# A list-scheduled kernel for a convolution, a spectral mixer and an fp8 MLP: pieces' durations taken from the trace, and the order of issue searched anew

## The chip, the cores and the metric

The kernel runs on one core of a Trainium2 chip. The metric is the time of one execution on the device in microseconds (us). A core has five engines that run side by side, each with its own queue of instructions worked off strictly in order: PE (matrix multiplications, results into PSUM), DVE (vector work), ACT (activations and copies), POOL (a slower vector engine) and SP (issues most of the DMA transfers here). They wait for each other through semaphores. [...]

## The reference

The input is 32 images of 56 x 56 pixels with 96 channels. For each image `reference()` computes two layers, all with weights shared by the images.

Layer 0, a convolution block with mixed experts:

```python
pooled = jnp.mean(x, axis=(1, 2))
rw = jax.nn.sigmoid(pooled @ Wr + br)                     # 4 mixing weights per image
h = relu(bn(x @ Wk + ...))        # Wk = sum_e rw_e Wpw_e, 96 -> 384 channels
h = relu(bn(cond_dw(h)))          # sum_e rw_e * depthwise 3x3 convolution
x = bn(h @ Wk2 + ...) + x         # Wk2 = sum_e rw_e Wpwl_e, 384 -> 96 channels
```

Layer 1, on the 3136 pixels as tokens: `t + attn(layernorm(t))`, and then `t + ffn(layernorm(t))`. The attn is a map from 96 to 192 channels with relu, an FFT over all 3136 tokens, a diagonal complex map with relu on the real and the imaginary part, the inverse FFT, its real part, and a map from 192 back to 96 channels. The ffn is a two-layer MLP (96 to 384 to 96) whose operands are rounded to an 8-bit float (5 exponent bits, 2 mantissa bits), with sums rounded to 16 bits.

## The kernel before

Every image is recorded by `record(b)` (line 767) as 572 small pieces of work, 118 of them on PE. A piece has an engine, an estimated duration, a due time, and the buffers and tiles that it reads and writes. `Plan.order()` (line 269) then runs a list scheduler over the pieces of all 32 images: whenever an engine of its model is free, it takes the ready piece with the earliest due time whose buffers can be had from their rings (PSUM banks are such a ring). The order in which pieces are taken is the order in which the program is written out (line 1477), and `Pinned` (line 370) keeps this order on every engine; so all instructions of the main part carry the line number 380. At run time the model's times have no meaning any more: an engine works off its queue in the written order and waits where an operand or a buffer isn't there yet.

What decides the order: `WANT` (line 173) with due times of the stages and the period between images, `NUDGE` (line 182), 572 numbers that are added to the due times, the same for every image, `HURRY` (line 176), subtracted from the due time of every DVE and ACT piece that reads PSUM, `LAG` and `DMA_LAG` (lines 156 and 162), the handoff times, `packets()` (line 165), the time of a transfer, and `slack`, a time by which a piece that reads a transfer is held back in the model after the transfer's modelled end. The order repeats from image to image once the pipeline is full; pieces of up to four images are interleaved.

The pieces of an image, by the names that this document uses (a number behind a name counts the pieces of that name within an image):

- *Convolution block.* `in` loads the image in four parts (SP), `pad` copies each into a padded tile (ACT). `route` (PE) makes the mixing weights; `wk`, `small` and `mix_wk2` (DVE) mix the expert weights, and `wd`, `wk2` rearrange them through DRAM (SP). The 384 channels are three chunks, the image two halves. Three of the six chunk-halves go "by vector": `expV` (PE), then nine taps as DVE and ACT pieces. The other three go "by tensor": `expT` (PE, four pieces), four transfers `hp` from SBUF to SBUF that regroup the channels, `conv` (line 990, PE, 64 matmuls in four phases), and four transfers `hid`. So there are `conv.0`, `conv.1` (first half) and `conv.2` (second half), with `hp.0` to `hp.11`. `proj.0` to `.2` and `.3` to `.5` (PE) project a half back to 96 channels, and `landed` (DVE) adds it to the image.
- *Forward part*, in four stretches of 14 rows: `turn` (PE transpose), `stats` and `rest` (DVE), `root` (line 1106, POOL) for the layer norm; `hidden` (PE), `scaled` (DVE), `along_h` (line 1173, PE, the transform along one axis), a copy on ACT, and transfers `gd` to DRAM. Each stretch has two groups, so there are `along_h.0` to `.7`.
- *Frequency part*, in seven groups of 4 or 5 frequencies: `g2` (line 1203) loads a group from DRAM, `along_q` (PE, two pieces per group) transforms along the other axis, nine pieces on ACT and DVE apply the diagonal map and the relu, `second` (line 1300, PE) maps 192 to 96 channels, `seconds` (ACT) copies it out, `back_q` (PE) transforms back, a copy, and `yd` stores it to DRAM.
- *Tail*, in four stretches again: `xs`, `yt`, `dd` are loads, `back_h` (line 1370, PE) transforms back along the first axis, which needs all seven `yd`; then `turn.4` to `.7`, `stats`, `rest`, `root` (POOL), `shift` (DVE), `normal` (line 1394, ACT), `turn_back` (line 1403, PE), a copy, and for each of three chunks `up` (line 1423, PE), a copy and a relu on ACT, a cast `h8` on POOL (line 1435), and `down` (PE); at last the sum and the store `out`.

Of the kernel before, what the change touches and what calls it, by code (L numbers as in the profile page):

```python
# [18 lines left out]
NE = 4  # L19
C = 96  # L20
# [144 lines left out]
def packets(n, size):  # L165
# [6 lines left out]

WANT = dict(period=113.9, half=60.1, expand=0.0, vector=1.4, forward=10.7, forward_step=27.0, freq=172.2,
            freq_step=7.0, tail=259.2, tail_step=26.5, x=17.0, mix=33.5, project=33.0)

HURRY = 666.0

# [4 lines left out]
NUDGE = [  # L182
    -172.8, -9.2, -163.5, -60.3, 106.2, -144.5, 5.2, 53.2, -138.8, -8.2, -18.1, 99.5, 147.5, 94.2, 30.4, 67.4, 92.4, -148.5,
    -6.5, -38.5, 17.2, -12.9, -15.4, -66.7, 8, 47.3, 43.1, -21, 54, 5.1, 79, 62.9, 70.9, 46, 65.8, 61.6,
    84.4, 85, 84.4, 40.6, -2.1, 87.1, 20.9, 22, 0.2, 78.2, 60.5, 28.6, 19, 81.3, 37.6, 57.2, 88.1, 56.4,
    66.3, 27.8, 87.7, 47.1, 3.9, -118.2, -64.2, -84.3, -87, 1.7, 38, -13.3, 3.3, 79.4, -68.9, 6.1, -39.3, -22.4,
    -19.6, 33.1, 71.9, 22.4, 90.3, 8.3, 105.6, -2.6, 53.5, -90.3, -62.6, -103.8, -44.5, 28.1, 84, 81.8, 41.1, 65.4,
    8.5, -38.6, -23.9, -6.9, 6.4, 31.1, 20.5, -24.2, -49.9, -25.7, -1.2, 35.9, 4.4, 29.3, 35.4, 31.7, 11.2, 32.7,
    -0.6, 2.9, 64.3, 55.4, 21.5, 6, 26.4, -13.2, -2.6, -11, -7.5, -46.8, -15.5, -65, -6.8, -1.4, -9.5, -61.2,
    -31.8, -58.5, 20.3, 11.2, -20.3, -4.1, -1.5, -38.9, -22.4, 22.3, 23.7, -10.1, 25.5, 18, -0.4, 34.1, 24.9, 15.9,  # L190
    16.3, -10.2, 31.4, 20, 22.3, 21.4, 68.6, 6.5, 20.6, 32.1, 45.3, 0.2, 87.8, 97.5, 26.2, 165.3, 25.8, 69.2,
    -2.3, 75.7, -13.1, 128.9, -49.1, -108.2, -48.2, -13.1, 8.1, -3, 25.2, 64.8, 93.3, -26.5, -18, -36.1, -44, 25,
    40.1, 17.9, -68.7, -67.4, -63.8, -83.2, 48.6, -63, 51.9, -62.9, 51.9, 52.1, -44.3, -24.4, -95.9, 11.6, 10.1, -125.8,
    -87.7, -2.9, -83.3, 1.2, -12.6, -52.9, -15.4, 74.6, -82.7, 30.3, -7, 42.3, 39.1, -114.4, 9.2, -95.3, 27.5, 21,
    -15.1, 18.2, 13.7, -47.5, 10, 15.9, -62.4, -63.7, 18.7, -75.9, 1.4, -102.1, 66, 13.6, -89.4, -47.9, -79.5, 7.9,
    27.8, -78.8, -48.7, -13.9, -80.9, 7.2, -17, -75.7, 2.9, 34.7, -79.6, 18.7, -29.5, -51.1, 29.1, -120.2, -27, -174.8,
    -19.6, -1.7, -101.7, -132.1, -25.7, -135.5, -3.1, -29.4, -68.3, -35, -106.8, -36.1, -32.9, -24.2, -19.8, -72.9, -51.2, -26.6,
    -193.3, -161, -26, -32.5, -13, -23, 2, -38.4, -26.7, -48.1, -139.2, -94.1, -29.8, -21.3, -65.4, -22.5, -55.3, -54.9,
    -104, 2.6, 50, -62.3, -1.2, -99.1, -50, -31.3, -93.3, -124, -30.2, 30.5, -6.3, -48.4, 9.1, -63.1, 23.9, -32.4,
    -123.4, -98.1, -13.4, -29.5, 2.9, -15.5, -54.1, -85.5, -81.5, -70, -65.3, -64.4, -9.9, -63.4, -67.9, -49.2, -238.5, -138.2,  # L200
    -51.4, -18.7, -39.4, -87.4, -30.3, -73.9, -33.3, -80.2, -229.8, -126.4, -52, -64, -103.4, -40.4, -65.3, -50.3, -83.5, -2.5,
    -2.7, -75.9, -43, -126.9, -9.5, -24.2, -129.6, -23.3, 4.8, 37.3, 44.5, 14.3, 64.3, -80.5, 24.6, -6, -141, -113.4,
    -0.5, -18.6, 6.6, -17.9, -90.6, -142.3, -89.1, -9.7, 39.2, 0.3, 64.2, -29.5, 14.3, 27.4, -160.3, -34.4, 20.7, 9.1,
    18.6, 19.1, 34, -87.3, 22.2, -20.8, -79.3, -114.3, -21, -1.7, -46.5, 1.5, -56.6, -68.3, -96, -11.4, 7.3, -31,
    -1, -113.3, -20.1, -2.5, -133.2, -104.9, -6.8, 32.5, -0.9, 15.3, 67.8, -62.8, 32.2, -0.4, -84, -89.1, 48.2, -11,
    9.3, 43.2, -1.5, -48, -40.4, 3.9, 40.7, -28.9, 46.7, -47.5, 12.9, 24.6, -140.4, -106.2, 23.3, 13.5, -12.4, 27.8,
    13.9, -47.3, -7.4, 5.3, -87, -93, 11.7, 18.1, -83.2, -13.4, -87, -74.7, 14.1, 53.6, 39.4, 15.6, -33.3, 7,
    -90, -14.5, -32.6, -58, -68.1, -127.6, 70.6, -91.1, -82, -120.2, -128, -95.6, -46.5, -198.2, -126.4, -74.2, -83.7, -138.5,
    -99, -84.9, -60.2, -28.1, 23.8, -92.6, 27.3, -29.5, -3, 14.7, 11.8, 22.6, 27.2, -37.4, -126.3, -32, -88.4, -49.7,
    -80.9, -115.3, 44.8, -36.2, -64.3, -126.9, -78.2, -25.2, -36.4, -46, -79, -23.3, -32.1, -93.1, -97.6, -15.3, -44.1, 7.2,  # L210
    69.9, -69, -43.9, 51.1, 2.7, 75.7, 49.8, 54.4, 62.2, -32.2, -53.4, 7.7, -51.1, -6.4, 24.5, -84.8, 136.4, -14.6,
    6.6, -88.3, -65, 0.9, -18.3, -70.5, -45.5, 2.6, -12.9, -65.1, -65.4, -0.1, -18.6, -23.2, 77.8, -37.1, 0.8, -7.6,
    5, 67.2, 25.4, 103.6, 150.3, 33.5, -55.5, 40.7, -47.9, 2.3, 49.7, -3.5, 176, 13.2, -18.2, -66.6, -65.7, -28.6,
    15.8, -58.1, 11, 16.7, -29, -88, -20.9, 33.5, -35.4, 17.5, 44.4, -13.1, 48.4, 59.1,
]
# [3 lines left out]
class Plan:  # L219
# [15 lines left out]

    def add(self, eng, dur, due, emit, reads=(), writes=(), takes=(), size=0, port=None):
        op = Op()
# [4 lines left out]
        op.eng, op.dur, op.due, op.emit = eng, dur, round(due, 3), emit  # L242
        op.takes, op.size, op.slack = list(takes), size, 0.0
        op.port = eng == "POOL" if port is None else port
# [141 lines left out]
def kernel(  # L386
# [56 lines left out]
    wpw_s = const([C + 1, NE + 1, M], F32, "wpw_s")  # L443
# [45 lines left out]
    with tc.tile_pool(name="prep", bufs=1) as pp:  # L489
# [4 lines left out]
        half = temp([128, 16], "half")  # L494
# [255 lines left out]
    add, move = plan.add, plan.move  # L750
# [16 lines left out]
    def record(b):  # L767
        t0 = b * PERIOD
        xh = [Buf(xr[h]) for h in range(2)]
        mix = Buf(r_mix)  # L770
        wk, small, wk2 = Buf(r_wk), Buf(r_small), Buf(r_wk2)
# [3 lines left out]
        for st in range(NS):  # L775
# [4 lines left out]
            else:  # L780
# [3 lines left out]
                    writes=[(sx, 0)], takes=[sx],  # L784
                )

            def pad(st=st, h=h, k=k, sx=sx):
# [6 lines left out]
            add(  # L794
                "ACT", 0.84, t0 - WANT["mix"] - 10 + 2 * st, pad, reads=[(sx, 0)], writes=[(xh[h], k), (mix, ("sum", st))],
                takes=[mix, *xh] if st == 0 else [],
            )
# [12 lines left out]
        def spread():  # L810
# [9 lines left out]
            reads=[(pooled, 0)], writes=[(psm, 0)], takes=[psm],  # L820
# [3 lines left out]
            reads=[(psm, 0)], writes=[(mix, 2)],  # L824
# [6 lines left out]
        def mixed(to, of, last, p):  # L831
            rw = mix.ap[0:p]
            for e in range(NE):
                ve.scalar_tensor_tensor(to, of[:, e], rw[:, e : e + 1], last if e == 0 else to, ALU.mult, ALU.add)

        def mix_wk2():
# [7 lines left out]
        add(  # L844
            "DVE", 3.08, t0 - WANT["mix"], lambda: mixed(wk.ap, wpw_s, wpw_s[:, NE], C + 1), port=True,
            reads=[(mix, 2)], writes=[(wk, 0)], takes=[wk],
# [3 lines left out]
            reads=[(mix, 2)], writes=[(small, 0)], takes=[small],  # L850
# [77 lines left out]
        def by_tensor(h, c, due, hid):  # L928
# [47 lines left out]
            def conv():  # L976
# [12 lines left out]
            add(  # L989
                "PE", 3.8, due, conv, reads=[(wg, 0), *((hp, r) for r in range(4))],  # L990
                writes=[(ps, r) for r in range(4)], takes=[ps],
# [83 lines left out]
        def moments(p, of, key, due, out_extra):  # L1075
# [29 lines left out]
            add("DVE", 0.52, due + 1, rest, writes=[(ln, 0)])  # L1105
            add("POOL", 1.78, due + 1, root, port=False, writes=[(ln, 0)])
            return ps, ln

        gd, yd, xd = Buf(r_gd), Buf(r_yd), Buf(r_xd)
        for st in range(NS):  # L1110
# [22 lines left out]
            for q0, nq in ((0, 4), (4, 3)):  # L1133
# [27 lines left out]
                def along_h(q0=q0, nq=nq, ps=ps, ha=ha, da=da):  # L1161
# [10 lines left out]
                add(  # L1172
                    "PE", 0.82, due + 3, along_h, reads=[(ha, 0), (da, 0)], writes=[(ps, 0)], takes=[ps, g],
                )
# [23 lines left out]
        for i, (k0, nk) in enumerate(GROUPS):  # L1198
# [6 lines left out]
                ),  # L1205
                reads=gd_parts, writes=[(g2, 0)], takes=[g2],
            )
# [80 lines left out]
            def second(nk=nk, nb=nb, ps=ps, za=zs[0], zb=zs[1]):  # L1288
# [10 lines left out]
            add(  # L1299
                "PE", 0.29 * nk + 0.1, due + 5, second, reads=[(zs[0], 0), (zs[0], 1), (zs[1], 0), (zs[1], 1)],  # L1300
                writes=[(ps, 0)], takes=[ps, zo],
# [38 lines left out]
        for st in range(NS):  # L1340
# [28 lines left out]

            add("PE", 1.43, due, back_h, reads=[(yt, 0), (dd, 0)], writes=[(ps, 0)], takes=[ps])  # L1370
            add(
# [21 lines left out]
            add("DVE", 0.1, due + 3, shift, writes=[(ln, 0)])  # L1393
            add("ACT", 2.1, due + 4, normal, reads=[(ps, 0), (ln, 0)], writes=[(nt, 0)], takes=[nt])
            ps, n8 = Buf(banks, 2), Buf(r_n8)
# [6 lines left out]

            add("PE", 0.55, due + 5, turn_back, reads=[(nt, 0)], writes=[(ps, 0)], takes=[ps, n8])
            add(
# [8 lines left out]
            for c in range(NC3):  # L1413
                ps, h16, h8 = Buf(banks, 2), Buf(r_h16), Buf(r_h8)

                def up(c=c, ps=ps, n8=n8):
# [5 lines left out]

                add("PE", 0.4, due + 7, up, reads=[(n8, 0)], writes=[(ps, 0)], takes=[ps, h16])
                add(
# [9 lines left out]
                add(  # L1434
                    "POOL", 0.79, due + 9.5,
                    lambda h16=h16, h8=h8: po.tensor_copy(h8.ap, h16.ap, saturate=False),
# [38 lines left out]
    for b in range(NB):  # L1475
        record(b)
    for op in plan.order():
        op.emit()


# [112 lines left out]
```

## Time and profile before

| | us |
|---|---|
| time before, median of 3 runs | 4395.16 (4389.32 to 4395.35) |
| profiled execution, its own time | 4390.8 |
| profiled execution, its span | 4389.0 |
| PE busy | 3988.9 (91%) |
| DVE busy | 3551.2 (81%) |
| ACT busy | 3110.9 (71%) |
| POOL busy | 1632.2 (37%) |
| main DMA queue, share of 16 engines | 64.8% |
| mean granted clock of PE | 0.950 |

A busy time is the time in which an engine worked on at least one instruction; the rest of the span it waited. The granted clock is the share of full speed at which PE was allowed to run: in a stretch at 0.5 a matmul takes twice its time, and the engine counts as busy meanwhile. A timeline line gives start, duration, engine, source line, operation, written and read tiles, shapes, the number of instructions in the group and, in brackets, the idle time before it with what ended it. All PE pieces come from line 380, so a piece is told by its tiles: `ps<-hp,wg` is `conv`, `ps<-dd,yt` is `back_h`, `ps<-ha,da` is `along_h`, `ps<-h,fw` is `down`.

### The profile page before, as it was taken

The page shows a single profiled execution, that of the slowest core. Times are in us where ns is not written, and L with a number is a line of the kernel's source. Part 1 is how long each engine was busy: PE and PEld are TensorE (multiplying, and loading weights), DVE is VectorE, ACT ScalarE, POOL GpSimd, SP SyncE. Part 2 cuts the span into 40 slices and gives each one's busy share as a digit, 9 for nine tenths or more (in the row PEclk, how much of TensorE's full clock was granted, in tenths as well). Part 3 has the DMA queues.
Part 4 walks back from the last instruction along what each step waited for, and adds up shares of the span by engine and source line. Part 5 has one row for each costly group of instructions (what it writes and reads, how often), then busy time and mean ns, then how long its engine had stood idle before and what let it go on. Part 6 is the DMA issues. An engine that isn't in the chain of part 4 may idle for free.

```text
span 4389.0 us, 104599 instructions
## 1 busy us (share of the span) xinstructions
PE 3988.9 (91%) x40066; PEld 2522.6 (57%) x40066; DVE 3551.2 (81%) x9036; ACT 3110.9 (71%) x6281; POOL 1632.2 (37%) x1332
## 2 busy tenths in 40 slices
PE   2888999999999999999999999999999999999985
PEld 0455655666565665655666655566565566665663
DVE  5877777798888889877888888888977888888853
ACT  1456766677777777766778777777876777877765
POOL 1223333333334434333333434433433333343333
PEclk9988999999999999999999999999999999999986
DMA  5754776666776666676666777666667666667642
GB/s 119 139 140 118 168 162 144 154 147 170 172 169 164 162 161 160 164 160 149 154 154 154 174 175 168 167 161 152 162 162 162 159 156 149 162 170 178 157 130 65
DMA packets 427749, 679.25 MB, mean 155 GB/s; under 512 B 155062, under 2 KB 290678, under 8 KB 427206
## 3 DMA queue, kind: packets, MB, share of 16 engines
q1 hardware_dynamic: 421632, 668.08, 64.8%
q8 instruction: 316, 5.18, 0.5%
q10 hardware_dynamic: 5618, 4.49, 0.4%
q14 instruction: 183, 1.50, 0.1%
HBM read 300.21 MB, written 211.04 MB: 116 GB/s over the span
## 4 chain that ended last, share of the span: by engine, by line
PE 46%; ACT 19%; DVE 13%; DMA 9%; POOL 6%; issue 4%; SPq 1%; POOLq 0%; ACTq 0%; DVEq 0%
PE ps L380 46%; ACT h L380 6%; ACT nt L380 5%; POOL ln L380 5%; DVE ln L380 3%; DVE ha L380 3%; ACT tmpa L380 2%; DMA hp<-h 2%; DMA yt<-yd 2%; DMA da<-dad 2%; DVE za L380 2%; DVE tmpa L380 2%; DVE h L380 1%; ACT tmpb L380 1%; ACT y L380 1%
## 5 line engine op out<-in xcount | busy, mean ns | idle before, releaser
L380 DVE SCALAR_TENSOR_TENSOR h<-h,small,h 128x784 f32<-128x784 f32 x1536 | 1557.0, 1050 | 103.3 <-ACT h L380 84.5
L380 POOL CAST h<-h 128x784 fp8e5<-128x784 f16 x384 | 511.2, 1335 | 738.3 <-ACT h L380 738.3
L380 PE MATMUL ps<-x,wk 97*32 97x435 f32 (+2 forms) x3840 | 698.7, 571 | 9.3 <-DVE wk L380 9.1
L380 POOL TENSOR_TENSOR ln<-ln,mhalf 120x7 f32<-120x7 f32 (+1 forms) x256 | 473.9, 1851 | 21.3
L380 PE MATMUL ps<-hp,wg 32*32 32x392 f32 x12288 | 420.4, 520 | 48.6 <-DMA hp<-h 28.1
L380 POOL TENSOR_SCALAR ln<-ln 120x7 f32<-120x7 f32 (+1 forms) x256 | 130.0, 508 | 866.4 <-DVE ln L380 866.4
L380 PE MATMUL ps<-dftb_s,g 112*128 112x112 f32 (+1 forms) x3776 | 432.1, 288 | 12.5 <-DVE tmpa L380 9.9
L380 ACT ACTIVATE h<-ps 128x435 f32<-128x435 f32 (+2 forms) x768 | 388.7, 543 | 69.8 <-PE ps L380 55.6
L380 PEld LDWEIGHTS ps<-dftb_s,g 112*128 112x128 f32 (+1 forms) x3776 | 353.3, 172 | 143.9 <-issue 41.9
L380 DVE SCALAR_TENSOR_TENSOR ha<-ps,ln,nshift 120x192 f32<-120x192 f32 x896 | 306.4, 408 | 155.7 <-PE ps L380 150.3
L380 DVE BATCH_NORM_STATS2 ln<-ps 120x6 f32<-120x96 f32 (+1 forms) x1792 | 315.8, 247 | 69.2 <-PE ps L380 68.5
L380 PEld LDWEIGHTS ps<-x,wk 97*32 97x32 f32 (+1 forms) x3840 | 203.6, 125 | 276.1 <-issue 141.9
L380 ACT ACTIVATE h<-h,fb 128x784 f16<-128x784 f16 x384 | 361.1, 965 | 1.3
L380 PEld LDWEIGHTS ps<-hp,wg 32*32 32x32 f32 x12288 | 218.7, 105 | 232.0 <-issue 106.9
L380 PE MATMUL ps<-w1c,x 96*120 96x192 f32 x1792 | 342.7, 342 | 6.6 <-issue 5.5
L380 ACT ACTIVATE nt<-ps,ln 112x96 fp8e5<-112x96 f32 x896 | 301.7, 436 | 62.6 <-DVE ln L380 58.7
L380 PEld LDWEIGHTS <-fw 96*128 96x128 fp8e5 (+1 forms) x1536 | 155.5, 115 | 315.7 <-issue 214.6
L380 ACT CAST h<-ps 128x784 f16<-128x784 f32 x384 | 308.7, 828 | 36.0 <-PE ps L380 34.5
L380 ACT ACTIVATE hp<-ps,small 128x392 f32<-128x392 f32 x384 | 202.1, 598 | 178.2 <-PE ps L380 163.0
L380 PEld LDWEIGHTS ps<-w1c,x 96*120 96x120 f32 x1792 | 301.7, 189 | 45.8 <-issue 29.8
L380 POOL TENSOR_TENSOR xs<-xs,y 96x784 f32<-96x784 f32 x128 | 238.1, 1860 | 238.6 <-DVE y L380 238.6
L380 PE MATMUL ps<-h,wk 32*96 32x392 f32 x3072 | 316.2, 496 | 2.8 <-DMA h<-hp 1.0
(171 smaller groups left out, 7313.0 us busy)
## 6 DMA issues: line engine op xcount, KB each, us to landing
hp<-h SPq DMA_DIRECT2D x384, 217.5 KB
h<-hp SPq DMA_DIRECT2D x384, 196.0 KB
gd<-g SPq DMA_DIRECT2D x384, 192.0 KB
g<-gd SPq DMA_DIRECT2D x192, 336.0 KB
dd<-ddd SPq DMA_DIRECT2D x128, 392.0 KB
yt<-yd SPq DMA_DIRECT2D x128, 336.0 KB
xd<-park SPq DMA_DIRECT2D x128, 294.0 KB
xs<-xd SPq DMA_DIRECT2D x128, 294.0 KB
```

The lines of the kernel that those rows point to most:

```text
L380: return self.tc.keep_in_program_order(method(*args, **kwargs))
```

## The change

No instruction of the computation is changed. The plan's numbers are: eight kinds of pieces get other durations, three kinds of pieces that read a transfer are held back longer in the model (for `add` could not take a `slack` before), `HURRY` grows, the period grows by 0.1, and all 572 numbers of `NUDGE` are new. From these `Plan.order()` writes out another order on PE, DVE, ACT, POOL and SP, and gives some buffers other places of their rings.

```diff
-WANT = dict(period=113.9, half=60.1, expand=0.0, vector=1.4, forward=10.7, forward_step=27.0, freq=172.2,
+WANT = dict(period=114.0, half=60.1, expand=0.0, vector=1.4, forward=10.7, forward_step=27.0, freq=172.2,
-HURRY = 666.0
+HURRY = 1060.2
 NUDGE = [
...
 ]
-    def add(self, eng, dur, due, emit, reads=(), writes=(), takes=(), size=0, port=None):
+    def add(self, eng, dur, due, emit, reads=(), writes=(), takes=(), size=0, port=None, slack=0.0):
...
-        op.takes, op.size, op.slack = list(takes), size, 0.0
+        op.takes, op.size, op.slack = list(takes), size, slack
...
                 "ACT", 0.84, t0 - WANT["mix"] - 10 + 2 * st, pad, reads=[(sx, 0)], writes=[(xh[h], k), (mix, ("sum", st))],
-                takes=[mix, *xh] if st == 0 else [],
+                takes=[mix, *xh] if st == 0 else [], slack=2.5,
...
-            "DVE", 3.08, t0 - WANT["mix"], lambda: mixed(wk.ap, wpw_s, wpw_s[:, NE], C + 1), port=True,
+            "DVE", 2.57, t0 - WANT["mix"], lambda: mixed(wk.ap, wpw_s, wpw_s[:, NE], C + 1), port=True,
...
-                "PE", 3.8, due, conv, reads=[(wg, 0), *((hp, r) for r in range(4))],
+                "PE", 3.75, due, conv, reads=[(wg, 0), *((hp, r) for r in range(4))],
...
-            add("POOL", 1.78, due + 1, root, port=False, writes=[(ln, 0)])
+            add("POOL", 1.95, due + 1, root, port=False, writes=[(ln, 0)])
...
-                    "PE", 0.82, due + 3, along_h, reads=[(ha, 0), (da, 0)], writes=[(ps, 0)], takes=[ps, g],
+                    "PE", 0.81, due + 3, along_h, reads=[(ha, 0), (da, 0)], writes=[(ps, 0)], takes=[ps, g],
...
-                reads=gd_parts, writes=[(g2, 0)], takes=[g2],
+                reads=gd_parts, writes=[(g2, 0)], takes=[g2], slack=3.5,
...
-                "PE", 0.29 * nk + 0.1, due + 5, second, reads=[(zs[0], 0), (zs[0], 1), (zs[1], 0), (zs[1], 1)],
+                "PE", 0.47 * nk - 0.45, due + 5, second, reads=[(zs[0], 0), (zs[0], 1), (zs[1], 0), (zs[1], 1)],
...
-            add("PE", 1.43, due, back_h, reads=[(yt, 0), (dd, 0)], writes=[(ps, 0)], takes=[ps])
+            add("PE", 1.44, due, back_h, reads=[(yt, 0), (dd, 0)], writes=[(ps, 0)], takes=[ps], slack=4.0)
...
-            add("ACT", 2.1, due + 4, normal, reads=[(ps, 0), (ln, 0)], writes=[(nt, 0)], takes=[nt])
+            add("ACT", 2.22, due + 4, normal, reads=[(ps, 0), (ln, 0)], writes=[(nt, 0)], takes=[nt])
...
-            add("PE", 0.55, due + 5, turn_back, reads=[(nt, 0)], writes=[(ps, 0)], takes=[ps, n8])
+            add("PE", 0.4, due + 5, turn_back, reads=[(nt, 0)], writes=[(ps, 0)], takes=[ps, n8])
...
-                add("PE", 0.4, due + 7, up, reads=[(n8, 0)], writes=[(ps, 0)], takes=[ps, h16])
+                add("PE", 0.36, due + 7, up, reads=[(n8, 0)], writes=[(ps, 0)], takes=[ps, h16])
...
-                    "POOL", 0.79, due + 9.5,
+                    "POOL", 0.82, due + 9.5,
```

The three held-back pieces are `pad` (after its `in` transfer), the move `g2` (after the `gd` transfers that it reads) and `back_h` (after `yt` and `dd`). In a settled image of the new order on PE, counted from `route`: `proj.0` to `.2` and `along_q.0` to `.2` stand before `conv.2`, not behind it; `back_h.3` comes directly behind `route` and `up.6`, `up.7` follow it; `up.8`, `down.6` to `.8` stand close together; `turn.6` and `turn_back.2` stand closer. From `back_q.6` over `conv.0` and `back_h.0` to `conv.1` the order is nearly the old one. On SP, `yt.0` is issued before `yt.1`; before it was behind it.

## The prediction

> **What bounds the kernel now.** I read the first page, then windows cut image by image, then the waits of PE, then the timelines of PE and of SP, and last the chain that ended last. The page:
>
> ```profile
> span 4389.0 us, 104599 instructions
> PE 3988.9 (91%) x40066; PEld 2522.6 (57%) x40066; DVE 3551.2 (81%) x9036; ACT 3110.9 (71%) x6281; POOL 1632.2 (37%) x1332
> ```
>
> PE is the bound: 91% of the span over 32 images, with DVE 10 points behind. But a share over the whole span hides that images differ. Windows from one `route` matmul (the first PE work of an image's conv block) to the next give about 126 us for a quick image and 133 to 140 us for others, with the same instructions. Here are a quick one, a long one, and a stretch of the second; the columns are window, length, busy time of PE, PEld, DVE, ACT, POOL with counts, granted clock, DMA share, GB/s:
>
> ```profile
> 1463.60:1590.20 126.60, 121.15 (x1252) 76.50 (x1252) 109.67 (x278) 96.68 (x197) 51.16 (x41) 0.99 0.70 166
> 1845.30:1984.80 139.50, 129.57 (x1253) 82.29 (x1253) 109.83 (x278) 96.90 (x198) 50.97 (x41) 0.93 0.65 150
> 1897.40:1908.00 10.60, 10.60 (x76) 8.00 (x77) 4.52 (x20) 3.49 (x6) 1.63 (x2) 0.52 0.55 113
> ```
>
> DVE, ACT and POOL do the same work in both; the 13 us are PE waits and PE work at half clock (0.52 for 10.6 us, some 5.1 us lost there). Over images 6 to 30 the excess above 126 us sums to 97 us, all in images 6 to 8, 13 to 17 and 22 to 27. Summing the shortest time of each of the 118 PE pieces of an image gives 113.5 us, so even a quick image loses 12 to 13 us. What ends these losses, from the waits of PE (total, times, longest):
>
> ```profile
> PE ps L380 <- ACT h L380: 61.6, 121, 2.1
> PE ps L380 <- issue: 49.0, 24, 4.1
> PE ps L380 <- DVE tmpa L380: 29.8, 64, 1.3
> PE ps L380 <- ACT zo L380: 29.3, 31, 1.3
> PE ps L380 <- DMA hp<-h: 28.1, 34, 4.1
> PE ps L380 <- DMA yt<-yd: 20.2, 11, 4.0
> ```
>
> No wait is long; there are many small ones, each tied to a place in the order. Two belong to transfers. `conv.2` in a quick image, then `back_h.0` in a long one (start, us, what, idle before and its releaser):
>
> ```profile
> 1534.72 1.52 PE L380 MATMUL ps<-hp,wg 32*32 32x392 f32 x24
> 1536.80 3.46 PE L380 MATMUL ps<-hp,wg 32*32 32x392 f32 x104 [0.56 <-DMA hp<-h]
> ```
>
> ```profile
> 1887.17 2.53 PE L380 MATMUL ps<-dd,yt 116*96 116x112 f32 x14 [1.72 <-DMA yt<-yd]
> 1890.28 3.81 PE L380 MATMUL ps<-hp,wg 32*32 32x392 f32 x106
> 1897.36 1.25 PE L380 MATMUL ps<-hp,wg 32*32 32x392 f32 x22 [3.27 <-issue]
> ```
>
> The chain that ended last passes through the same place, `yd.6`, `yt`, `back_h.0`:
>
> ```profile
> 1870.03 6.78 DMA yd<-y
> 1877.25 9.78 DMA yt<-yd
> 1887.17 6.92 PE ps L380 x118
> ```
>
> and the issues of SP there show what stands before that `yt`: four `hp`, `yd.6`, four `hp`, `xs.0`, `wd`, then `yt.1` and `yt.0`, the last two in one line:
>
> ```profile
> 1741.21 0.58 SPq L380 DMA_DIRECT2D yd<-y  x1
> 1741.89 2.47 SPq L380 DMA_DIRECT2D hp<-h  x4
> 1744.41 0.58 SPq L380 DMA_DIRECT2D xs<-xd  x1
> 1745.93 0.34 SPq L380 DMA_DIRECT2D wd<-wkc  x1
> 1747.95 2.10 SPq L380 DMA_DIRECT2D yt<-yd  x2
> ```
>
> **The change part by part.** Durations, slack and nudges only feed the planner: no instruction is added or removed, and PE's pieces still sum to 113.5 us an image. What changes is who stands between a producer and its consumer. I call the PE work between the two the cover, and hold it against the time that the trace shows for the chain. Images 5 to 31, 27 of them, run in the settled order; fill and drain keep their order of PE work, so they are counted at nothing (bounds: 5 us either way, a twentieth of an image's fill).
>
> *1. conv.2.* The cover from its last `expT` to `conv.2` goes from 6.9 to 17.6 us, as `proj.0` to `.2` and `along_q.0` to `.2` now come first. `conv.0` and `conv.1` have 14.3 and 16.3 us and do not wait. Above, `conv.2` takes 5.54 us (1534.72 to 1540.26) against 3.70 undisturbed; median over quick images 2.07 us lost. Gain 2.1. `proj.0`, moved earlier, needs `hid.4` to `.7`, which land 10 to 11.5 us after `conv.1`; its cover falls from 27.7 to 22.3, still enough, so nothing is late there.
>
> *2. back_h.0.* Between `back_q.6` and it PE's cover is unchanged, 18.6 us, and it starts 0.1 us after `yt.0` lands in all images. SP now issues `yt.0` before `yt.1`. In the trace the second starts 0.5 us later and lands 0.8 later. `yt.1` has 14.7 us to spare. Gain 0.8; ends 0 and 1.7 (all of the wait shown).
>
> *3. along_h.0 to .3.* Cover behind `hidden` 1.83, 1.62, 6.78, 1.55 becomes 3.39, 2.24, 2.90, 2.36. The `scaled` pieces between take 306.4/896 = 0.34 us per 192 columns, 1.4 for four, plus handoffs. The pieces lose 0.77+0.45+0.26 = 1.5 today. Gain 1.5; ends 0.7 and 1.5.
>
> *4. second.2 and back_h.3.* Behind `second.2` the next piece waits 1.15 us (the row of ACT zo, 31 times, one an image). `back_h.3` now stands directly behind `route`, ahead of the `second` pieces. Gain 1.15; its successor is 5.
>
> *5. second.3* now has 2.96 us of cover behind `along_q.7`; the chain of ACT and DVE pieces between them took 4.4 us where it was shortest. Loss 1.4; ends 0.9 and 1.8.
>
> *6. turn_back.2.* Cover behind `turn.6` falls from 13.8 to 6.5 us. The chain is stats, rest, root (POOL), shift, normal. From the rows by form: stats 158.9/128 = 1.24, root (259.3+70.7)/128 = 2.58, normal 301.7/128 = 2.36; with rest 0.6 and handoffs of 0.4 to 1 it is 7.2 to 7.8. The shortest such chain of the trace is 7.1 (tail 0), with root at 1.79; root's longest is 3.47, which makes 9.1. Loss 1.2; ends 0.6 and 2.6. Behind it PE's queue stops whole, as it is in order: `back_q.4`, `turn.1` and the next image's `route` stand there.
>
> *7. down.8* has 3.6 us behind `up.8`; the chain (copy 0.83, relu 0.97, cast on POOL 1.34, handoffs, POOL busy with another cast) took 4.5. Loss 0.9; ends 0.5 and 1.3.
>
> *8. g2.0.* It is now issued behind four `hp` (870 KB) and `in.2`. `along_q.0` had 5.7 us to spare; 870 KB at the quick image's 166 GB/s take 5.2. Loss 0.5; ends 0 and 2. The other `g2` keep 2 us or more except `g2.6` (0.3), inside those ends.
>
> *The rest.* Busy time of DVE, ACT, POOL: the same pieces, queues of like length; hidden under PE as before. `in` loads start 10 to 20 us earlier, which moves DMA load, and no consumer of it was near.
>
> [...]
>
> Sum for an image: gains 2.1+0.8+1.5+1.15 = 5.55, losses 1.4+1.2+0.9+0.5 = 4.0, net -1.55. Over 27 images -42 us. The profiled execution took 4390.8 us (span 4389.0), which is 4.4 under the median of 4395.16; 4390.8-42 = 4349, on the median's footing 4353. I say 4352.
>
> Best ends: gains 6.45, losses 2.0: -4.45, -120 us, 4275. Worst: gains 3.95, losses 7.7: +3.75, +101 us, 4496.
>
> **The rivals.** *A: the long images go as well.* They begin where `back_h.0` waits 1.7 us, or shortly behind it. If 0.8 us less is enough, up to 97 us more go: 4352-97 = 4255. For: the wait of 1.72 us stands just ahead of the drop of the clock. Against: 3.27 us of the loss at 1897.36 is "issue", for which no transfer of the kernel is the cause, and PE's order there is the same.
>
> *B, slower: the new wait at turn_back.2.* If it comes near its upper end of 2.6 us it is longer than the 1.72 us that stood before half clock in the trace, and it lies in a stretch with other short waits. One drop costs 5.1 us (row at 1897.40). Without part 6 the sum is -2.75; so part 6 decides from 2.75 us an image on: a wait of 2.6 and a drop in one image of thirty is break-even, a drop in half of the images makes 2.6+2.55-2.75 = +2.4, or +65 us, 4460. For: tail 2's root runs on POOL beside casts of 1.34 us, and DVE holds taps of 1.05 us ahead of stats. Against: the chains of tails 0 and 3 take 7.1 and 8.4.
>
> [...]
>
> *C: gains eaten, no change.* Waits only move: about 4390. A measurement of this kernel can tell about 0.2% (9 us) from no change.
>
> **How the numbers follow.** My forecast 0.39, A 0.13, B 0.40, C 0.08. So faster 0.52, same 0.08, slower 0.40. The likeliest alone: 4310 to 4385. The range leaves out a tenth on either side: low 4250 (A), high 4465 (B).
>
> **What would show it.** `conv.2` in 3.7 us without the DMA hp wait; the row DMA yt below 10 us; along_h near 0.88 each; new waits at `second.3` (DVE tmpa) and `turn_back.2` (ACT nt). Quick images at 124 to 125 us would prove the sum; 128 or more, or half clock behind `turn_back.2`, would prove B; no image above 130 would prove A. I am wrong altogether if a chain that I took as hidden, most likely a `g2`, now stops PE in each image.

## The result and the profile after

The changed kernel takes 4324.94 us (median of 4 runs, 4320.91 to 4334.73), the kernel before 4392.24 us in the runs beside it; the ratio is 0.9851 with a 95% interval of 0.9831 to 0.9871. The forecast was 4352. The sign, the range and roughly the size (-67 us against -43) hold. The steps that the sum was made of do not hold as well, as the rest of this document shows. The first page of the changed kernel's profile:

```profile
span 4319.1 us, 104500 instructions
PE 3856.5 (89%) x40066; PEld 2445.1 (57%) x40066; DVE 3615.6 (84%) x9036; ACT 3084.7 (71%) x6281; POOL 1662.0 (38%) x1332
```

PE's busy time fell by 132 us and its idle time grew by 62. That split misleads: a matmul group that waits in its middle counts as busy (`conv.2` took 5.5 us before with 3.7 us of work), so busy time is not work. Windows by image tell more. Two images of the changed kernel from `route` to `route`, a quick one and a long one (columns as in the prediction):

```profile
2196.62:2322.10 125.48, 117.60 (x1253) 74.73 (x1253) 111.72 (x279) 96.31 (x198) 51.63 (x41) 0.97 0.71 168
1666.37:1803.10 136.73, 124.36 (x1255) 79.65 (x1253) 112.40 (x279) 96.24 (x196) 52.69 (x42) 0.93 0.66 153
```

The quick image is where it was: the median distance from one `back_h.0` to the next over images 8 to 28 is 127.3 us, and it was 127.8. So the forecast gain of 1.55 us in every image is not there. Where the 70 us of the profiled span went is seen from the absolute starts of pieces. `conv.0` of image 8 starts at 1075.6 us and not 1114.2: 39 us come from the fill. From there to `back_h.0` of image 28 another 41 us go. What were the long images 13 to 17 and 22 to 27 are some 56 us shorter, and some 13 us are lost again in two places where images are long now (133 to 137 us). The sum of what images 6 to 27 take above 126 us falls from 85 to 50 us. The last images give 10 us back: image 28 alone takes 140 us, and with it the sum is 64.

The waits of PE after (total, times, longest):

```profile
PE ps L380 <- DVE zb L380: 76.9, 86, 3.5
PE ps L380 <- ACT y L380: 55.3, 56, 1.1
PE ps L380 <- ACT h L380: 48.1, 67, 3.4
PE ps L380 <- ACT g L380: 26.4, 30, 0.9
PE ps L380 <- ACT nt L380: 24.9, 34, 4.3
PE ps L380 <- issue: 24.4, 17, 3.4
PE ps L380 <- DMA yt<-yd: 21.5, 23, 1.8
```

The rows of `hp`, `tmpa` and `zo`, which headed the list before, are gone or small. In their place stand rows that were at 3.7, 2.3 and 0.5 us before: `zb`, `ACT y`, `ACT g`. I put the start of each PE piece that runs in the quick images 9 to 12 and 18 to 21 (from `route` to `route`) beside the shortest time that a piece of its kind takes in either trace; what is left over is lost time, put down to the piece after which it is lost (medians):

| lost in front of or within | before | after | prediction |
|---|---|---|---|
| `conv.2` | 2.13 | 0.04 | -2.1 |
| `second.2` and the piece behind it | 1.15 | 0.00 | -1.15 |
| `back_h.0` | 0.78 | 1.20 | -0.8 |
| `along_h.0`, `.1`, `.3` | 1.81 | 1.27 | -1.5 |
| `second.3` | 0.00 | 0.35 | +1.4 |
| `turn_back.2` | 0.00 | 0.00 | +1.2 |
| `down.8` | 0.00 | 0.00 | +0.9 |
| `along_q.0` (`g2.0`) | 0.00 | 0.00 | +0.5 |
| `second.5` | 0.00 | 1.71 | none |
| `second.0` | 0.09 | 1.60 | none |
| `route` | 0.00 | 1.30 | none |
| `turn_back.1` | 0.00 | 1.06 | none |
| `down.6` | 0.06 | 0.85 | none |
| sum over all 118 pieces | 19.4 | 19.8 | -1.55 |

Of the 1.27 behind the `along_h` pieces after, 0.92 is no wait of theirs but that of `second.4`, which now follows, for a PSUM bank (row `ACT g`). The 0.85 at `down.6` is no wait either: in 12 of 21 images the piece in front of it, `expV.0`, runs at half clock behind the wait of `second.5` and takes 1.91 us instead of 1.05. Two of the four gains came as forecast. That behind `along_h` was smaller, and that at `back_h.0` isn't there in quick images: over images 7 to 28 its mean wait falls from 1.16 to 0.80 us, and what goes are the waits over 1.2 us, nine before and two after, most of them in long images. Of the four losses one came, at `second.3`, with a quarter of its size; and four waits that I had not listed came in their place.

### The profile page after: what moved, and what is told of

It reads as the page before. It is cut to its first block, busy times and chain, and to the rows that moved or that the text cites. A ratio compares the mean times of both kernels' runs of the same rounds, so it can differ in the third digit from the quotient of the medians.

```text
span 4319.1 us, 104500 instructions
## 1 busy us (share of the span) xinstructions
PE 3856.5 (89%) x40066; PEld 2445.1 (57%) x40066; DVE 3615.6 (84%) x9036; ACT 3084.7 (71%) x6281; POOL 1662.0 (38%) x1332
## 4 chain that ended last, share of the span: by engine, by line
PE 36%; DVE 28%; ACT 17%; DMA 10%; issue 5%; SPq 1%; POOL 1%; POOLq 0%; DVEq 0%; ACTq 0%
PE ps L380 36%; DVE h L380 8%; DVE ln L380 5%; ACT nt L380 5%; DMA yt<-yd 5%; ACT h L380 4%; DMA yd<-y 3%; DVE ha L380 3%; DVE za L380 3%; DVE zb L380 2%; DVE wk L380 2%; DVE tmpb L380 2%; ACT tmpa L380 2%; DVE tmpa L380 1%; ACT za L380 1%
## 5 line engine op out<-in xcount | busy, mean ns | idle before, releaser
L380 POOL CAST h<-h 128x784 fp8e5<-128x784 f16 x384 | 582.4, 1521 | 1430.5 <-ACT h L380 1427.8
L380 PE MATMUL ps<-dftb_s,g 112*64 112x112 f32 (+1 forms) x3776 | 433.5, 288 | 18.4 <-DVE ln L380 14.3
L380 POOL TENSOR_TENSOR ln<-ln,mhalf 120x7 f32<-120x7 f32 (+1 forms) x256 | 421.1, 1645 | 21.3
L380 PEld LDWEIGHTS ps<-dftb_s,g 112*64 112x64 f32 (+1 forms) x3776 | 352.1, 173 | 131.1 <-issue 62.1
L380 DVE BATCH_NORM_STATS2 ln<-ps 112x6 f32<-112x96 f32 (+1 forms) x1792 | 318.5, 250 | 112.6 <-PE ps L380 112.5
L380 PE MATMUL ps<-hp,wg 32*32 32x392 f32 x12288 | 382.1, 512 | 21.9 <-issue 15.0
L380 ACT ACTIVATE hp<-ps,small 128x392 f32<-128x392 f32 x384 | 215.8, 601 | 230.6 <-PE ps L380 210.6
L380 POOL TENSOR_TENSOR xs<-xs,y 96x784 f32<-96x784 f32 x128 | 275.1, 2149 | 266.3 <-DVE y L380 263.2
L380 ACT ACTIVATE h<-h 128x784 f32<-128x784 f32 x192 | 164.4, 858 | 174.8 <-DVE h L380 173.4
L380 PE MATMUL ps<-h,wkc 128*96 128x392 f32 x768 | 284.9, 519 | 0.0
```

The costliest lines, as they stand in the source:

```text
L380: return self.tc.keep_in_program_order(method(*args, **kwargs))
```

## The experiments

All are edits of the order of issue alone, apart from the runs on durations and nudges and the run on one cast. The computation is whole in all of them. Each kernel that moves pieces takes the written-out order, moves the named pieces on the queue of their engine, and merges the queues again so that every piece still follows what it needs.

**1. The swap alone, on the kernel before.** On SP's queue `yt.0` goes before `yt.1`, in every image:

```diff
-    for op in plan.order():
+    # yt.0 directly before yt.1 on SP's queue, same image
+    for op in merged(plan.order(), ((445, 0, "before", 477, 0, 0, 31),), len(NUDGE), NB):
         op.emit()
```

> The kernel before, with one edit on the queue of SP: in every image yt.0 is issued directly before yt.1, as in the changed kernel. Theory (the long images start at the wait of back_h.0 for yt.0): the wait at back_h.0 becomes 0.4 to 0.9 us shorter in every image, the streaks of long images become shorter as in the changed kernel, and the time falls by 30 us or more (4362 or less). Rival (the streaks come from the place of back_h.0 and conv.1 in the order and from the late instruction fetch, not from yt.0): the time falls by 0 to 15 us and the images 14 to 17 and 24 to 27 stay at 132 us or more.

Measured 4310.49 us, ratio 0.982 (0.979 to 0.985) against the kernel before: 85 us less, by one swapped pair of transfers. That is no less than the whole change brought. `yt.0` lands 20.68 us behind the start of `back_q.6` (median), and 21.62 before: 0.94 us earlier. Rows of PE's waits in this run (in the prediction the same rows stand at 49.0 and 20.2):

```profile
PE ps L432 <- issue: 20.4, 15, 2.7
PE ps L432 <- DMA yt<-yd: 7.9, 5, 2.6
```

In quick images `back_h.0` waits no more. The long images 14 to 17 and 24 to 27 take 126 to 130 us now, but for two at 136 and 133 us, and the excess above 126 us of images 6 to 28 falls from 85 to 41. The fill gains too: `conv.0` of image 8 at 1089.3.

**2. The swap undone, on the changed kernel.**

```diff
+    # yt.1 directly before yt.0 on SP's queue, same image
+    for op in merged(plan.order(), ((477, 0, "before", 445, 0, 0, 31),), len(NUDGE), NB):
```

> The changed kernel, with the one edit undone: yt.1 is issued directly before yt.0, as in the kernel before. Theory: back_h.0 waits 0.4 to 0.9 us longer in every image, the streaks of three to four long images return, and 20 to 35 us of the gain are lost (4345 to 4360). Rival: within 10 us of the changed kernel's 4325.

Measured 4403.41 us (4391.07 to 4444.56), ratio 1.0034 (1.0007 to 1.006) against the kernel before. So the whole gain hangs on this pair: all the rest of the change, without it, leaves the kernel no faster (8 us slower by the medians). The wait is 2.0 us longer per image than with the swap (0.8 and 2.8 us, means of images 7 to 28), where I had taken 0.8. The row of waits, and one `back_h.0`:

```profile
PE ps L432 <- DMA yt<-yd: 77.4, 29, 3.7
```

```profile
2015.48 1.91 PE L432 MATMUL ps<-dd,yt 116*96 116x112 f32 x14 [3.26 <-DMA yt<-yd]
```

`yt.0` lands at 23.06 and not 20.95 us. Two transfers of 336 KB that start 0.4 us apart do not land 0.4 us apart: the second lands 0.8 us behind the first in the order of the kernel before and 1.8 to 1.9 in that of the changed kernel (medians with either of them first; 0.8 to 2.9 in single images). What sets the distance was not tested.

**What a wait at that place costs.** The six profiles of before, after, and the experiments 1 to 4 give 22 images each (7 to 28) with different waits in front of `back_h.0`. I took the clock lost in the 24 us from there on as (1 - granted clock) x 24 us, leaving out the 29 of the 132 images where PE ran dry once more for 0.5 us or more within 14 us:

| wait at `back_h.0` | images | clock lost, mean |
|---|---|---|
| under 1.2 us | 81 | 0.0 us |
| 1.2 to 1.6 us | 6 | 0.6 us |
| 1.6 to 2.0 us | 1 | 0.0 us |
| 2.0 to 2.6 us | 4 | 1.6 us |
| over 2.6 us | 11 | 2.3 us |

So at this place a wait of 0.9 us costs itself, and one of 2 us or more costs 1.6 to 2.3 us besides. The swap takes the kernel before from the second kind to none in the long images, and the undone swap puts nearly every image of the changed kernel there. By the table the losses at this place begin between 1.2 and 2 us. Where PE ran dry a second time (most of all by rows "issue" of 2 to 4 us within `conv.1`), more is lost, 2.3 to 6.8 us. The limit is that of this place and no rule for the kernel: in the changed kernel half clock followed the wait of `second.5`, at most 1.59 us, in 15 of 22 images, and that of `turn_back.1`, 0.90 us, in 6 of 23. One of them, and the stretch behind it (the last column but two is the clock, 0.50):

```profile
3727.03 0.64 PE L380 MATMUL ps<-w2b,zb 64*112 64x96 f32 x8 [1.59 <-DVE zb L380]
```

```profile
3728.11:3734.94 6.83, 6.83 (x29) 4.09 (x28) 3.74 (x9) 3.73 (x8) 4.11 (x4) 0.50 0.01 3
```

Over the images 6 to 28 the stretches of half clock behind `second.5` last 89 us, so about 44 us are lost there (at half clock matmuls of one piece start about twice as far apart: those of `back_h` 187 ns and not 96, medians of the changed kernel). A row "issue" within `conv.1` in the changed kernel:

```profile
1724.57 3.50 PE L380 MATMUL ps<-hp,wg 32*32 32x392 f32 x109
1730.83 1.20 PE L380 MATMUL ps<-hp,wg 32*32 32x392 f32 x19 [2.76 <-issue]
1731.95 4.84 PE L380 MATMUL ps<-w1c,x 96*120 96x192 f32 x14
```

The trace has one packet of 16 KB on an instruction queue at 1728.36 us, inside this gap, and others at the like gaps at 696 and 1864 us. All gaps of that kind over 1.5 us (nine before, six in the changed kernel, four in experiment 1) have such a packet under way, or one that began at most 1.3 us before; with 316 packets in a run, about a third would by chance. And the place within `conv.1` at which PE stops moves on by 13 to 15 matmuls from one image to the next (104 and 117 in images 4 and 5 of the kernel before, 106 and 119 in 14 and 15, 108 and 121 in 24 and 25), so the gaps come back every ten images, as the streaks do. That instructions came late would fit all this, but it is a guess that no run shows; the cause stays open. Why the swap shortens the streaks of long images from four to one or two the traces show in part: in the long images 13 to 15 and 23 to 25 of the kernel before, `yt.0` lands 2.2 to 2.5 us behind `yt.1` and not 0.8; in experiment 1 the distance there is the same, but then it is `yt.1` that is late, which has 13 us to spare.

**3. Four pieces of DVE moved, on the changed kernel.** The new waits of `second.5` and `second.0` are for DVE. The timeline of PE in the changed kernel, and that of DVE at the same time (`zb` is written last by `d5.11`):

```profile
2202.28 0.81 PE L380 MATMUL ps<-zo,dftc_s 112*112 112x384 f32 x2
2204.36 0.64 PE L380 MATMUL ps<-w2b,zb 64*112 64x96 f32 x8 [1.27 <-DVE zb L380]
```

```profile
2199.75 0.62 DVE L380 SCALAR_TENSOR_TENSOR wk<-wpw_s,mix 97x384 f32<-97x384 f32 x1
2200.41 2.38 DVE L380 SCALAR_TENSOR_TENSOR wk<-wpw_s,mix,wk 97x384 f32<-97x384 f32 x3
2202.71 0.26 DVE L380 SCALAR_TENSOR_TENSOR zb<-tmpb,zb 128x112 f32<-128x112 f32 x1
2202.89 0.90 DVE L380 TENSOR_TENSOR ln<-ln 120x7 f32<-120x7 f32 x2
2204.04 0.27 DVE L380 SCALAR_TENSOR_TENSOR zb<-zb,tmpb 128x112 f32<-128x112 f32 x1
```

The two short pieces that `second.5` needs (0.26 and 0.27 us) stand behind `wk`, 3 us, and `rest.1`, 1.2 us, which nobody on PE needs as early. The edit puts them in front:

```diff
+    MOVES = (
+        (411, 0, 'before', 14, 2, 3, 29),     # d4.11 before wk of the image after next
+        (412, 0, 'after', 411, 0, 3, 29),     # d5.11
+        (282, 0, 'before', 297, 0, 3, 31),    # d5.1 before d4.2
+        (272, 0, 'before', 297, 0, 3, 31),    # d5.0 before d4.2
+    )
```

> The changed kernel with four pieces moved on the queue of DVE: d4.11 and d5.11 go in front of wk, d5.0 and d5.1 in front of d4.2. second.5 and second.0, which wait for them 1.6 and 1.3 us in nearly every image, should start without a wait. Theory (waits of PE add up, PE is the bound): 2.5 to 3 us an image less, quick images near 123.5 us, 4245 to 4265. Rival (a wait that goes comes back at the next PE piece that DVE or ACT feeds): less than 20 us, quick images stay at 126.

Measured 4258.12 us, ratio 0.9699 (0.9667 to 0.9732) against the kernel before, and 67 us below the changed kernel. This version beats both. The median image takes 124.8 us and not 127.3; of the 2.9 us lost at `second.5` and `second.0` that were taken away (1.71 to 0.05 and 1.60 to 0.34), 2.5 stayed away. The number came as expected, but the length of the waits is not all that was won: PE's idle time fell by 28 us only, and 41 of the 52 us between the profiled spans are half clock that is gone (the table behind experiment 10). `second.5` in this run:

```profile
2177.44 0.81 PE L432 MATMUL ps<-zo,dftc_s 112*112 112x384 f32 x2
2178.18 0.64 PE L432 MATMUL ps<-w2b,zb 64*112 64x96 f32 x8
```

**4. The wait of conv.2 brought back, on the changed kernel.** `hp.8` to `.11` go behind `in.3` of the next image on SP's queue.

> The changed kernel with the four transfers hp.8 to hp.11 moved on the queue of SP from ahead of in.2 to behind in.3 of the next image, about 11 us later. conv.2 should wait for them again, by 2 to 4 us an image. Theory (waits of PE add up): the time grows by about what conv.2 waits, 26 images x 2 to 4 us, 4375 to 4430. Rival (such a wait lets DVE and ACT run ahead, and later waits of PE shrink by the same): less than half of what conv.2 waits is seen in the time.

Measured 4451.02 us, ratio 1.0142 (1.011 to 1.0175): 126 us more than the changed kernel. That is above the range I had given. `conv.2` takes 4.7 us longer, and the piece before it 1.6; the median image takes 130.9 us, 3.6 more. But most of this is not a wait: of the 8.4 us that `conv.2` takes here 6.8 are at half clock, where in the kernel before it took 5.5 us with no half clock in 20 of 23 images (medians of images 6 to 28). The profile's first page fits that:

```profile
span 4442.0 us, 104524 instructions
PE 3983.9 (90%) x40066; PEld 2480.9 (56%) x40066; DVE 3606.2 (81%) x9036; ACT 3088.2 (70%) x6281; POOL 1654.8 (37%) x1332
```

The span is 123 us longer and PE's idle time is not (458 us, and 463 in the changed kernel). The mean granted clock fell from 0.954 to 0.932, which makes up to 105 of the 123 us. And as the other theory said, waits elsewhere fill with work: `second.0` loses 0.20 us and not 1.60, `down.6` 0.2 and not 0.9. So it is not shown that waits add up one by one. Nor is it shown that part 1 of the prediction, the 2.1 us at `conv.2`, was worth its length in the changed kernel: the loss brought back here is another one, at half clock.

**5. route moved behind back_h.3, on the version of experiment 3.**

> The run with the four DVE pieces moved (4258 us), with one more piece of PE moved: route goes behind back_h.3, since in its place it waits 1.1 us for the copy of back_q.4 (ACT y) in nearly every image; the DVE and ACT pieces that follow route (radd, sig) move back by three and one places. Theory (waits of PE mostly add up): 0.8 to 1.1 us an image less, 4225 to 4240. Rival (wk comes later and holds the expansions up): 4250 to 4275.

Measured 4271.48 us: 13 us slower than without the move. The rival's time, but not its reason. `back_h.3`, now in front, waits 1.65 us where `route` waited 1.30: it needs a pair of PSUM banks that a layer-norm piece on DVE has not yet let go (the releaser is DVE ln). The row of that wait was 22.5 us in experiment 3 and is

```profile
PE ps L432 <- DVE ln L432: 61.5, 62, 3.1
```

**6. Three more PE moves on top.** `along_q.0` before `turn_back.1`, `up.4` behind `along_q.2` and `up.3` behind `conv.2`, `down.6` and `.7` next to `down.8`.

> As the run with route moved, and in addition: along_q.0 before turn_back.1 (which waits 1.0 us for ACT nt), up.4 behind along_q.2 and up.3 behind conv.2 (0.9 us, ACT h), down.6 and down.7 to just before down.8 (1.0 us, POOL cast). Theory (waits of PE mostly add up): 2 to 3 us an image less than the run with route moved, 4160 to 4190. Rival (the waits come back at the next pieces of the same chains, up.3 to down.3, down.8 to xsout): within 20 us of the run with route moved.

Measured 4420.03 us, 149 us slower than experiment 5, outside of what either theory expected. The wait at `up.4` went (1.07 to 0.10), that at `down.6` too (1.01 to 0.17), but `second.0` waits 4.1 us. ACT tells why:

```profile
2324.60 0.44 ACT L432 ACTIVATE zb<-ps,fb 128x112 f32<-128x112 f32 x1
2328.70 0.81 ACT L432 CAST h<-ps 128x784 f16<-128x784 f32 x1 [3.66 <-PE ps L432]
2329.40 0.69 ACT L432 ACTIVATE tmpb<-ps,fb 128x112 f32<-128x112 f32 x2
```

```profile
2334.87 1.06 PE L432 MATMUL ps<-w2b,zb 64*112 64x96 f32 x8 [3.82 <-DVE zb L432]
```

The copy of `up.3` keeps its place on ACT's queue. With `up.3` behind `conv.2` it stands there for 3.66 us with its operand missing, and the pieces that feed `second.0` stand behind it. So a PE piece moved without its consumers blocked the consumers' queue, for 3.66 us here. The other moves were not run one by one, so what each is worth stays open.

**7 and 8. One half of the plan's numbers at a time.** First the new durations and held-back landings with the old `NUDGE`, `HURRY` and period, then the reverse.

> The durations and held-back landings of the change with the old NUDGE, HURRY and period. Its order has yt.1 before yt.0 as the kernel before has, but conv.1 and two hidden pieces stand between back_q.6 and back_h.0. If yt.0 and the clock drop behind it are what counts, the longer cover at back_h.0 removes the wait and the streaks of long images, and the time is below 4350. If the searched nudges are what counts, an order that was not searched is slower than the kernel before: 4400 to 4500.

> The old durations and no held-back landings with the new NUDGE, HURRY and period. Its order has yt.0 before yt.1, but only behind the last of the hp transfers. If the nudges alone carry the gain, 4300 to 4360; if they fit only the durations that they were searched with, slower than the kernel before, 4400 to 4500.

Measured 4860.20 us (ratio 1.1075, 1.102 to 1.113) and 4762.21 us (1.0852, 1.0804 to 1.0899). In both many rows of PE's waits grow, `ACT h` to 88.5 and 95.4 us at the head, and none of them alone explains the time. The nudges fit only the durations that they were searched with; truer durations with the old nudges bring nothing. The change of `HURRY` does nothing: the changed kernel with the old 666.0 writes out the same order, piece by piece.

**9. The one long cast of the fill, on the kernel before.** In the first tail PE waits 10.6 us for a cast on POOL. Timelines of POOL, DVE and PE in the kernel before:

```profile
326.73 13.69 POOL L380 CAST h<-h 128x784 fp8e5<-128x784 f16 x3
```

```profile
327.51 11.43 DVE L380 SCALAR_TENSOR_TENSOR h<-h,small,h 128x784 f32<-128x784 f32 x12
```

```profile
339.69 0.81 PE L380 MATMUL ps<-h,fw 128*96 128x392 fp8e5 x2 [10.62 <-POOL h L380]
```

Of the three casts two take 0.83 us and the middle one 12.12: it begins with DVE's run of twelve taps, at 327.51 us, and ends 0.7 us behind the run's end (339.63 and 338.94 us). The edit does that one cast on ACT:

```diff
+                    if here:      # b == 0 and st == 0 and c == 1
+                        se.activation(h8.ap, h16.ap, AF.Copy, saturate=False)
+                    else:
+                        po.tensor_copy(h8.ap, h16.ap, saturate=False)
```

> The kernel before, with one single cast of the first image (h8.1, first tail stretch) done on ACT and not on POOL. In the kernel before this cast takes 12.1 us, not 0.84, while DVE runs twelve taps back to back, and PE waits 10.6 us for it, once. Theory (POOL stands still beside a long run of taps, and the wait is on the path of the fill): the wait of 10.6 us is gone, conv.0 of image 8 starts 8 to 11 us earlier (1103 to 1106 us and not 1114), the time falls by about that, 4381 to 4387. Rival (the next cast on POOL, h8.2, is caught in the same run of taps): PE waits about as long one piece later, and nothing is gained.

Measured 4381.20 us, ratio 0.9976 (0.9958 to 0.9994): 12 us less, and `conv.0` of image 8 at 1097.6 us. The wait is gone. The next cast was caught in the same run (8.68 us for two casts), as the rival said, but PE did not need it then.

**10. xs.0 behind yt.1, on the version of experiment 3.**

> The run with the four DVE pieces moved (4258 us), with one more edit on the queue of SP: xs.0 is issued behind yt.1 and no longer ahead of yt.0, so that 294 KB less are under way when yt.0 starts. Theory (every part of a us that yt.0 lands earlier, until back_h.0 waits no more, is worth more than itself, as the swap of yt.0 and yt.1 was): yt.0 lands 0.5 to 1 us earlier, back_h.0 waits 0.4 us or less and not 0.9, 10 to 35 us less, 4223 to 4248. Rival (the transfers do not share the queue in that way, or xs.0, which has 2.5 us to spare, now comes late): within 8 us of 4258 or slower.

Measured 4257.80 us (4239.87 to 4272.55) against 4258.12: no change. The wait of `back_h.0` went as expected, `yt.0` landing 1.3 us earlier:

```profile
PE ps L432 <- DMA yt<-yd: 4.1, 4, 1.4
```

It was 19.9 us in experiment 3. But of the 0.93 us an image 0.54 come back within `conv.1` and 0.28 at `second.0`. `conv.1` does not wait for its operands there, as its `hp` had landed 2.8 us or more before it; the cause stays open. It agrees with the table of waits: at `back_h.0` there is no clock to win under 1.2 us, and the rest depends on the next piece.

**What half clock makes of these differences.** (1 - mean granted clock) x span gives the most that half clock can cost in a profiled execution; a part of it falls on idle time. By this measure, in us:

| profile | span | half clock, at most |
|---|---|---|
| before | 4389.0 | 222 |
| changed kernel | 4319.1 | 198 |
| 1, the swap alone | 4315.7 | 181 |
| 2, the swap undone | 4389.3 | 236 |
| 3, four pieces of DVE | 4266.9 | 157 |
| 4, `conv.2` waits again | 4442.0 | 304 |
| 5, `route` | 4279.0 | 159 |
| 6, three more moves | 4418.2 | 236 |
| 7, old nudges | 4871.3 | 507 |
| 8, old durations | 4768.5 | 466 |

Of the 70 us that the change brought, 23 are clock at most; of the two swaps' 73 and 70, 41 and 38; of experiment 3's 52, 41; of experiment 4's 123, 105; of the 482 and 380 us that experiments 7 and 8 are slower, 285 and 245. A sum of waits does not hold this part, and it may be half or more of what experiments 1 to 4 moved.

## Why the prediction was right, and where not

- **The total** came out as forecast in sign and range, but that is luck in good part, as the 1.55 us an image that made it do not exist: quick images lose 19.8 us after and lost 19.4 before. The gain lies in the long images and in the fill. Three of its signs failed: quick images do not take 124 to 125 us, the row DMA yt stands at 21.5 us and not below 10, and `turn_back.2` does not wait.
- **Part 2 (yt.0 before yt.1)** is the term that was mis-sized: "Gain 0.8", 22 us in all, against 85 us in experiment 1 and 78 in experiment 2. Two things were missing. The distance of two landings in quick images (0.8 us) was taken as what a swap moves in all; in the new order it moves 2.1, and in the long images 13 to 15 and 23 to 25 of the kernel before, the same trace already had 2.2 to 2.5. And a wait was priced at its own length, where at this place one over some 1.2 us costs clock as well. The lower end of this part, 0, is shown by no run: the first of the two landed first in every one of the images 7 to 28 of the four profiles, by 0.8 to 2.9 us.
- **Rival A (the long images go as well)** is partly what happened; I had given it 0.13. Its mechanism, 0.8 us less at `back_h.0`, is shown by experiments 1 and 2; its objection, that the "issue" gaps would stay, holds for one or two images a streak, and its sign, no image above 130 us, did not come (images of up to 140 us are left).
- **Parts 1, 3 and 4** were right in kind. The losses at `conv.2` and `second.2` went, to within 0.05 us of the forecast, though that they shortened the time is not shown; behind the `along_h` pieces 0.5 are won and not 1.5, as a new wait came in their place.
- **Parts 5 to 8**, 4.0 us of losses, came to 0.35, at `second.3`. I counted cover in PE work. The time between two pieces also holds the waits of the pieces between, so a cover short by 1 us in work was not short in time. `turn_back.2`, on which rival B rested, waits 0.00 us. Part 8 does not follow from its own figures either: 5.7 us to spare less 5.2 of transfers leaves 0.5 us, not a loss of 0.5.
- **What the sum lacked** are four new waits, at `second.5`, `second.0`, `route` and `turn_back.1`, of about 5.6 us together, and half clock behind them (0.85 us at `expV.0`, which shows at `down.6`). They were hidden in the sentence on the rest: "queues of like length; hidden under PE as before". Length was not the point; what stands in front of the short pieces in the queue was. Experiment 3 shows it for two of the four: four moves on DVE, 67 us, a large part of it clock.
- **The fill** was counted at nothing with 5 us either way, since the order of PE work is the same there; 39 us came from it. It has the largest single waits: 10.6 us for one cast (experiment 9: 12 us), up to 3.0 us at `back_h.0` and 3.5 within `conv.1` of the first images. With the swap alone `conv.0` of image 8 comes 25 us earlier (experiment 1); with the swap undone on the changed kernel it comes at 1085.4 us, 10 later. How the rest of the 39 us divides was not separated.

## What to carry to other kernels

Ask first for the longest single waits in front of the bounding engine and for what lies just ahead of the awaited transfer in its queue; one swapped pair was worth no less than 572 searched numbers. When an order changes, read the queues of the engines that feed the bound, piece by piece, for a short piece that is needed soon behind a long one that is not; a cover counted in busy time tells neither a new wait nor the lack of one. Read the granted clock of each version beside its waits: what a wait cost here was its length and the clock behind it (1.6 to 2.3 us more for waits over 2 us at `back_h.0`). Move a piece together with its consumers: `up.3`, moved without its copy in experiment 6, blocked ACT's queue for 3.66 us.

## What the runs showed of the hardware

- In front of `back_h.0` a single wait of PE under 1.2 us cost no clock on average over 81 images (1.4 us in one of them); over 2 us it cost 1.6 to 2.3 us more than itself. Elsewhere half clock followed a wait of at most 1.59 us at `second.5` in 15 of 22 images, and one of 0.90 us at `turn_back.1` in 6 of 23.
- A cast on POOL of 0.84 us took 12.1 us beside twelve DVE instructions (`h<-h,small,h`, 128x784) back to back (11.4 us). Both began at 327.51 us, and the cast ended 0.7 us behind the last of the twelve. What held it was not tested.
- Two transfers of 336 KB issued 0.4 us apart landed 0.8 us apart in one order of the kernel and 1.8 to 1.9 us apart in the other (medians), and up to 2.9 us in single images.
